# A graph message-passing layer on one core: slots ranked up to 110 chunks ahead, shorter last segments, and a new hand-over between steps

## The chip, the cores and the metric

The kernel runs on one core of a Trainium2 chip. Its instructions are spread over five engines that run side by side, each through its own queue in order: PE (matrix products), DVE (vector arithmetic), ACT (activations), POOL (GpSimd; here it issues the scattered writes) and SP (which here issues nearly all other DMAs). The metric is the time of one execution on the device, in microseconds; the median of several runs is compared. One further execution is recorded by the profiler, and takes longer than the others.

## The reference

Only what matters is kept. There are 12500 nodes of 128 features and 412500 edges sorted by `dst`; `src` is in no order.

```python
h = jnp.maximum(_layernorm(x, axis=-1), 0.0)
h = h @ W_in2f                                        # per node
Wij = ssp(edge_attr @ W_f1 + b_f1) @ W_f2 + b_f2      # per edge, 20 -> 128 -> 128
x_ij = h[dst] * (Wij * edge_weight[:, None])          # per edge
agg = segment_sum(x_ij, src, num_segments=12500)      # per node
out = x + ssp(agg @ W_o1 + b_o1) @ W_o2 + b_o2        # ssp(z) = softplus(z) - log 2
```

## The kernel before, in words

**Tiles and chunks.** The edges are cut into groups of 2048 and chunks of 512 (`CH`); there are 202 groups (`NG`) and 806 chunks (`NCH`). One round of the main loop, `step(k)`, works on chunk k and on its neighbours: it finishes message k, prepares chunk k+1 and starts the first stages of chunks up to six ahead. The program writes the order of every engine's instructions out by hand (`manual_schedule`): an instruction stands in its engine's queue where the Python code emits it. Pools of buffers set the waits: a tile name with `bufs=4` may be written again only when the readers of its fourth last use are done.

**Gathering h[dst].** `make_h` (L317) normalizes four tiles of 128 nodes at a time, multiplies by `W_in2f` and stores the product as three bfloat16 parts in DRAM (L369). As `dst` is sorted, a chunk needs only 32 neighbouring nodes. `rows` (L599) loads these as `near`; `window` (L741) compares on DVE where each edge falls, giving `at`; `pick` (L768) multiplies `at` by `near` on PE and so gives each edge its row; `picked` (L775) copies it on ACT into `hg`, scaled by the edge's weight (L780).

**The edge filter.** For two chunks at a time `hidden` (L648) multiplies the 20 attributes by `W_f1` into `z` and runs Abs and Exp on ACT; `hidden_log` (L660) runs Ln; `hidden_end` (L664) adds the positive part on DVE, giving `r`. `bias` (L748) writes the bias of the second layer into PSUM by an ACT copy (L757), and `value` (L760) adds `r @ W_f2` to it on PE. `v` and `picked` share three PSUM buffers.

**Scattering.** `message` (L784) multiplies `v` by `hg` on DVE into `o` (L791; four buffers of two chunks each), and POOL writes the rows of `o` with four indirect DMAs per chunk (L795) to a table in DRAM, `slots`. Each row goes to a slot of the block of 128 nodes to which its `src` belongs. The slot is found by counting: `blocks` (L671) makes a one-hot matrix of each edge's block on DVE, `rank` (L679) adds it to running counts on PE (`free`, L692, and L725 for the chunk before), `rank_end` (L696) reduces them on DVE (`top`, L697), and three small DVE operations make the slot (L717 to L721). Before, this is done six chunks ahead of the message (`LR`).

**Segments and sums.** The groups are dealt into segments (`SEGS`), each with its own table of `T` tiles of 128 slots per block (one more for blocks that hold the chunk's own nodes). Tables are cleared by SP beforehand (L1099). When a segment's last message is nine steps old, `Collect` starts: it loads tiles of the table (`m`, L833), compares each row's place with 0 to 127 on DVE (`to`, L844), multiplies on PE (`acc`, L857), and adds each four blocks ("a quad") to `agg` in SBUF (L880). These units are dealt over the steps by a plan of rates in the program, up to step 811. The sums of the last segment come behind the loop, together with `finish` (L397): for each quad `agg @ W_o1` on PE, four passes on ACT (L385, L386, L394, L395), on DVE the sum `r` (L420), `x + b_o2` (L423), on PE `r @ W_o2` (L427), on DVE the last sum (L431), and the store of the result.

**Queues.** Loads and stores share SP's queue, so a DMA that waits for a buffer or for data holds those behind it. On DVE, message k stands behind `blocks`, `hidden_end` and `window` of later chunks; on PE, the picks of chunk k+1 stand behind its values.

Of the kernel before, what the change touches and what calls it, by code (L numbers as in the profile page):

```python
# [22 lines left out]
SEGS = (88, 40, 30, 14, 14, 8, 8)  # L23
# [6 lines left out]
UT = 6  # L30
# [11 lines left out]
def gnn_kernel(  # L42
# [38 lines left out]
    class Segment:  # L81
# [4 lines left out]
        def __init__(self, k):  # L86
# [7 lines left out]
            mean = (SEGS[k] * TG * P - (own[1] - own[0])) / QT * P / N  # L94
# [32 lines left out]


    tables = [(0, QN)]
# [4 lines left out]
    for c in range(NC):  # L134
        n = c * CH * N // n_edges
        table_of.append(0 if n < QN - NEAR - P else min(n // QN, NQ - 1) + 1)
# [4 lines left out]
    bf1, nbf1, bo1 = (sbuf(n, [P, 1]) for n in ("bf1", "nbf1", "bo1"))  # L141
# [10 lines left out]
    bf12 = sbuf("bf12", [P, P])  # L152
    zero = sbuf("zero", [P, ZR * RW])
# [27 lines left out]
    def load_x(q):  # L181
        n = min(QT, NTILE - q * QT)
        full = min(n, N // P - q * QT)
        xb = ln.tile([P, QT, P], F32, name="xb")
        if full < n:
            nc.vector.memset(xb[:, full:n, :], 0.0)
            nc.sync.dma_start(xb[:N % P, full, :], x[q * QN + full * P:N, :])
        if full:
            nc.sync.dma_start(xb[:, :full, :], x[q * QN:q * QN + full * P, :]
                              .rearrange("(c p) f -> p c f", p=P))  # L190
        return xb
# [59 lines left out]

    def constants():
# [3 lines left out]
        first_load(0)  # L256
        nc.sync.dma_start(win, w_in2f)

        for j in range(NCHUNK):
            nc.sync.dma_start(wf1[32 * j:32 * j + RBF, :], w_f1)  # L260

        nc.scalar.preload_act_table_set("natural_log_exp_and_others")
        nc.scalar.dma_start(bf1, b_f1[:, None])
        nc.scalar.dma_start(wf2, w_f2)
        nc.scalar.dma_start(bf2, b_f2[None, :].to_broadcast([P, P]))
        make_identity(nc, ident)
        for _ in bounds(0, nc.gpsimd):
            pass

        prow_i = early_room[:WP, rows_at + 5 * NC:rows_at + 5 * NC + 1].bitcast(I32)  # L270
# [6 lines left out]
                                pattern=[[1, P]], channel_multiplier=-1)  # L277
        nc.gpsimd.memset(zero, 0.0)
# [8 lines left out]
        nc.vector.memset(bad, 0.0)  # L287
        nc.vector.memset(rel[:, NPART - 1, :], 0.0)
        nc.vector.memset(ones, 1.0)
        nc.vector.memset(none, 0.0)  # L290

        for t in range(QT):
            nc.vector.memset(turn[:, :, t:t + 1], -1.0 if t % 2 else 1.0)
        nc.vector.tensor_scalar(prow_i, prow_i, 7, None, op0=ALU.logical_shift_right)
        nc.vector.tensor_copy(prow, prow_i)
# [3 lines left out]

    def biases(psum):  # L300

        nc.vector.tensor_scalar(nbf1, bf1, -1.0, None, op0=ALU.mult)
        b12 = psum.tile([P, QT, P], F32, name="b12", tag="acc")[:, 0, :]
        nc.tensor.matmul(b12, bf1.to_broadcast([P, P]), wf2, start=True, stop=True)
        nc.vector.tensor_add(bf12, b12, bf2)

    def late_loads():
        nc.sync.dma_start(wo1, w_o1)
# [5 lines left out]
    quads = []  # L314


    def make_h(q, psum):  # L317

        n = min(QT, NTILE - q * QT)
        xb = early.pop(q, None)  # L320
        if xb is None:
            xb = load_x(q)
# [41 lines left out]
        for (b, rows), table in zip(tables, h3_t):  # L364
            lo = max(0, b - q * QN) // P
            hi = min(n, (b + rows - q * QN) // P)
            if lo < hi:
                r = q * QN + lo * P - b
# [3 lines left out]
                if b + rows == QN:  # L372
                    yield
            if q == NQ - 1:
# [4 lines left out]
            h3[q * QN:q * QN + n * P, :].rearrange("(c p) f -> p c f", p=P),  # L379
            hb[:, :n, :, :].rearrange("p c k f -> p c (k f)"))  # L380
        yield
# [15 lines left out]
    def finish(t0, n, sT, quad, psum):  # L397
# [13 lines left out]
        yield  # L411

        z = psum.tile([P, 2, CH], F32, name="z_out", tag="z")[:, 0, :n * P]
# [3 lines left out]
        softplus_parts(a_n, r_n, z, bo1)  # L417
        softplus_logs(a_n)
        yield
        nc.vector.tensor_add(r_n, r_n, a_n)  # L420
        for p, cs, rows in pieces:
            xi = xo[:p, cs, :]
            nc.vector.tensor_add(xi, xi, spread(bo2[:p, :], xi.shape[1]))  # L423
        yield
        v = psum.tile([P, QT, P], F32, name="v_out", tag="v", bufs=3)
# [92 lines left out]
    with tc.tile_pool(name="edge", bufs=2) as edge, tc.tile_pool(  # L518
# [46 lines left out]
        class Group:  # L565


            def __init__(self, g):
# [3 lines left out]
                if g % NB == 0:  # L572
                    f = edge.tile([P, NB, CH], F32, name="f")
                    for j in range(NCHUNK):
                        nc.sync.dma_start(f[32 * j:32 * j + RBF, :, :],
                                          f_t[g:g + NB, j].rearrange("b k n -> k b n"))
                    kept["f"] = f
                self.f = kept["f"][:, g % NB, :]
                i = g - self.seg.g0
                if i % SB == 0:  # L580
                    w = min(SB, ceil_div(self.seg.c1, NCHUNK) - g) * TG
                    cols = slice(g * TG, g * TG + w)
                    src_i = edge.tile([P, SB * TG], I32, name="src_i")
                    nc.sync.dma_start(src_i[:, :w], src_t[:, cols])
                    rcut = edge.tile([P, SB * TG], F32, name="rcut")
                    nc.sync.dma_start(rcut[:, :w], rcut_t[:, cols])
                    kept["cols"] = [w, src_i, rcut]
                self.cols = kept["cols"]
                self.at = slice(i % SB * TG, (i % SB + 1) * TG)
                if g == 0:  # L590
                    rel_store(0)
# [620 lines left out]
```

## Time and profile before

| | |
|---|---|
| median of 3 runs | 4227.72 us (4224.9 to 4232.52) |
| profiled execution | 5772.48 us |
| its span | 5770.8 us |
| busy in it: PE, DVE, POOL, ACT | 3877.3, 3382.9, 3103.5, 2715.3 us |
| first scatter starts | 29.44 us |
| last scatter starts | 5625.94 us |
| granted TensorE clock, mean | 0.718 |

Rows of the timeline give start, duration, engine, line, operation, output <- inputs, and in brackets how long the engine was idle just before and what ended the wait. "issue" means that nothing the profile shows was waited for; "remote" that the releaser could not be named. Rows of groups give the count, busy time, mean duration and the idle time in front. PE's durations are modelled by the profiler.

### The profile page before, as it was taken

To read this page: it belongs to the slowest core of one execution; us is meant where nothing else is said; L and a number is where in the kernel's file an instruction comes from. 1 tells how busy PE (TensorE), PEld (TensorE's weight loads), DVE (VectorE), ACT (ScalarE), POOL (GpSimd) and SP (SyncE) were. 2 spreads that over 40 slices of the span, in tenths; PEclk is the share of its full clock that TensorE was granted. 3 is DMA by queue.
4 is the path that set the end of the run, shared out by engine and by line. 5 is a ranking of instruction groups with operands and counts; after the bars stand their busy time and mean duration, and the time that the engine had idled before them with its cause. 6 is when DMAs were issued, how large, how long until landed. Compare 5 with 4: busy or idle time off the path is not lost. (4 is left out here: it accounts for less than half of the span.)

```text
span 5770.8 us, 71871 instructions
## 1 busy us (share of the span) xinstructions
PE 3877.3 (67%) x21576; PEld 2912.2 (50%) x21576; DVE 3382.9 (59%) x6726; ACT 2715.3 (47%) x5490; POOL 3103.5 (54%) x3244
## 2 busy tenths in 40 slices
PE   5556555556555555577777777777777777777778
PEld 3333333333333333356655666566566665655557
DVE  5555555555444444466665666666666666566767
ACT  4455554555444444444444444444444444444444
POOL 5555555555555555555555555555555555555550
PEclk7665566565556566578777787788877788787879
DMA  5444443343333333255664554655555555555547
GB/s 150 138 135 141 130 141 119 115 137 104 99 89 87 106 109 87 82 152 161 188 183 137 158 160 144 190 163 157 160 168 173 154 150 178 165 141 153 145 126 215
DMA packets 515581, 820.80 MB, mean 142 GB/s; under 512 B 177074, under 2 KB 312870, under 8 KB 515186
## 3 DMA queue, kind: packets, MB, share of 16 engines
q1 hardware_dynamic: 411586, 602.85, 37.4%
q0 software_dynamic: 103168, 213.15, 11.2%
q8 instruction: 176, 2.88, 0.2%
q14 instruction: 219, 1.79, 0.1%
q10 hardware_dynamic: 432, 0.13, 0.0%
HBM read 419.09 MB, written 396.64 MB: 141 GB/s over the span
## 5 line engine op out<-in xcount | busy, mean ns | idle before, releaser
L795 POOL DMA_INDIRECT slots<-o,slot x3224 | 3100.3, 962 | 2522.6 <-DVE o L791 1605.2
L764 PE MATMUL v<-wf,r 128*128 128x128 f32 x6448 | 1209.4, 345 | 527.4 <-ACT a L657 207.3
L857 PEld LDWEIGHTS acc<-to,m 128*128 128x128 f32 x8132 | 1249.1, 238 | 577.1 <-issue 280.8
L857 PE MATMUL acc<-to,m 128*128 128x128 f32 x8132 | 1342.0, 329 | 271.0 <-DVE agg L880 136.4
L764 PEld LDWEIGHTS v<-wf,r 128*128 128x128 f32 x6448 | 1077.6, 251 | 850.7 <-issue 301.8
L780 ACT ACTIVATE hg<-picked,rcut 128x128 f32<-128x128 f32 x3224 | 913.1, 365 | 1256.6 <-remote 801.2
L697 DVE TENSOR_REDUCE top<-free 128x4 f32<-128x392 f32 x806 | 451.5, 560 | 1650.5 <-remote 990.2
L757 ACT ACTIVATE v<-bf 128x512 f32<-128x512 f32 x804 | 478.0, 595 | 1212.9 <-DVE o L791 888.5
L653 PE MATMUL z<-f,wf 20*128 20x512 f32 x1612 | 661.1, 881 | 406.9 <-DVE r L668 242.4
L844 DVE TENSOR_TENSOR to<-count_ps,m 128x512 f32<-128x512 f32 (+3 forms) x824 | 644.7, 806 | 255.3 <-remote 109.3
L772 PE MATMUL picked<-near,at 96*128 96x128 bf16 x3224 | 398.5, 257 | 495.3 <-ACT hg L780 317.4
L668 DVE SCALAR_TENSOR_TENSOR r<-z,nbf,a 128x1024 f32<-128x1024 f32 x403 | 516.2, 1281 | 242.3 <-ACT a L662 136.3
L656 ACT ACTIVATE a<-z,bf 128x1024 f32<-128x1024 f32 x403 | 454.0, 1127 | 400.4 <-remote 267.8
L772 PEld LDWEIGHTS <-at 96*128 96x128 bf16 x3224 | 315.5, 118 | 558.1 <-issue 531.3
L791 DVE TENSOR_TENSOR o<-v,hg 128x512 f32<-128x512 f32 x806 | 547.8, 680 | 16.8 <-ACT hg L780 12.8
L744 DVE TENSOR_TENSOR at<-count_ps,rel 96x512 bf16<-96x512 f32 x806 | 545.3, 677 | 0.0
L653 PEld LDWEIGHTS z<-f,wf 20*128 20x128 f32 x1612 | 174.6, 241 | 620.9 <-issue 428.9
L662 ACT ACTIVATE a<-a,half 128x1024 f32<-128x1024 f32 x403 | 468.1, 1162 | 0.0
L673 DVE TENSOR_TENSOR inb<-count_ps,blk 128x392 f16<-128x392 f32 x806 | 445.9, 554 | 0.0
L657 ACT ACTIVATE a<-a 128x1024 f32<-128x1024 f32 x403 | 425.8, 1057 | 12.8
L725 PE MATMUL free<-inb,rest_of 128*128 128x392 f16 x806 | 335.3, 416 | 117.6 <-issue 46.9
L692 PE MATMUL free<-inb,after 128*128 128x392 f16 x806 | 335.9, 417 | 17.4 <-issue 13.6
(108 smaller groups left out, 1142.5 us busy)
## 6 DMA issues: line engine op xcount, KB each, us to landing
m<-slots SPq DMA_DIRECT2D x311, 387.0 KB
m<-slots SPq DMA_DIRECT2D x317, 258.0 KB
rel<-rel_d SPq DMA_DIRECT2D x202, 384.0 KB
m<-slots SPq DMA_DIRECT2D x172, 322.5 KB
slots<-o,slot POOLq DMA_INDIRECT x3224
slots<-zero SPq DMA_DIRECT2D x96, 387.0 KB
slots<-zero SPq DMA_DIRECT2D x64, 516.0 KB
f<-in_f_t SPq DMA_DIRECT2D x404, 80.0 KB
```

The costliest lines, as they stand in the source:

```text
L653: nc.tensor.matmul(z[:, k, :], wf1[rows, :], self.f[rows, :], start=True, stop=True)
L662: nc.scalar.activation(a, a, AF.Ln, bias=half, scale=0.5)
L668: nc.vector.scalar_tensor_tensor(r, z, nbf1, a, op0=ALU.max, op1=ALU.add)
L744: nc.vector.tensor_tensor(at, prow_ps.to_broadcast([WP, CH]), self.rel[:, c, :], op=ALU.is_equal)
L757: nc.scalar.activation(v, spread(bf12, QT), AF.Copy)
L764: nc.tensor.matmul(v[:, i, :], r[:, i * P:(i + 1) * P], wf2, start=False, stop=True, skip_group_check=True)
L772: nc.tensor.matmul(ps[:, i, :], at[:, i * P:(i + 1) * P], near, start=i == 0, stop=i == QT - 1, skip_group_check=True)
L780: nc.scalar.activation(hg[:, i, :], ps[:, i, :], AF.Copy, scale=self.rcut[:, j:j + 1])
L791: nc.vector.tensor_mul(o[:, :, :P], v, hg)
L795: put = nc.gpsimd.indirect_dma_start(out=views[j % VIEWS], out_offset=bass.IndirectOffsetOnAxis(ap=self.slot[:, j:j + 1], axis=0), in_=o[: ...
L844: nc.vector.tensor_tensor(to[:, :n, :], count_ps[:, None, :].to_broadcast([P, n, P]), self.m[u][:, :n, P:].to_broadcast([P, n, P]), op=ALU ...
L857: nc.tensor.matmul(self.acc[b // QT][:, i, :], m[:, j, :P], to[:, j, :], start=t == 0, stop=t == self.seg.tiles(b) - 1)
```

## The change

Ranking is cut loose from the rest of a chunk. A new class `Places` holds what concerns slots (columns, `blocks`, `rank`), `Group` the rest. `ahead(k)` says how far ranking has come at step k: about six chunks ahead in the first rounds, then rising by a quarter to half a chunk per step up to 110 (`LEAD`), so that the last 110 steps have no ranking. Buffers for slots and places grow accordingly. `free`, the PSUM bank of the counts, becomes a second bank for `acc` when ranking is over (`sums_tile`).

The nine segments end in 3, 3 and 4 groups, where seven ended in 8 and 8. Loads of sums have at most four tiles (`UT`) and nine buffers; the compares take buffers from the pool of `make_h`. The plan of rates gives the last 110 steps half as much again.

Within a step, the message comes first. `picked` gets two PSUM buffers of its own and is filled two chunks ahead; `v` gets one. The bias of `v` is added by a PE matmul of a bfloat16 matrix with three rows of ones on the bias in three bfloat16 parts. Abs, Exp and Ln of `hidden` run together, one step after `z`. At the start the first tile of 128 nodes goes through `make_h` alone, then three, then four each; loads and constants come in another order, some from ACT's queue. In `finish`, the bias `b_o1` is folded in (`nbo1`; `b_o1 @ W_o2` is added to `b_o2`), one ACT pass and one DVE pass less are needed, and `x + b_o2` moves to GpSimd.

```diff
-SEGS = (88, 40, 30, 14, 14, 8, 8)
+SEGS = (88, 41, 25, 18, 12, 8, 3, 3, 4)
+LEAD = 110
-UT = 6
+UT = 4
+    made_h = [(0, 1), (1, QT - 1)]
+    made_h += [(t, min(QT, NTILE - t)) for t in range(QT, NTILE, QT)]
...
     def finish(t0, n, sT, quad, psum, tag="v", bufs=3, z=None):
+        for p, cs, rows in pieces:
+            xi = xo[:p, cs, :]
+            nc.gpsimd.tensor_add(xi, xi, spread(bo2[:p, :], xi.shape[1]))
...
-        softplus_parts(a_n, r_n, z, bo1)
+        nc.scalar.activation(a_n, z, AF.Abs, bias=bo1)
         softplus_logs(a_n)
         yield
-        nc.vector.tensor_add(r_n, r_n, a_n)
-        for p, cs, rows in pieces:
-            xi = xo[:p, cs, :]
-            nc.vector.tensor_add(xi, xi, spread(bo2[:p, :], xi.shape[1]))
+        nc.vector.scalar_tensor_tensor(r_n, z, nbo1, a_n, op0=ALU.max, op1=ALU.add)
...
+            def hidden_log(self, c):
+                z = self.pair[c]
+                a = quad.tile([P, 2, CH], F32, name="a", bufs=2)
+                nc.scalar.activation(a, z, AF.Abs, bias=bf1)
+                nc.scalar.activation(a, a, AF.Exp, scale=-1.0)
+                nc.scalar.activation(a, a, AF.Ln, bias=half, scale=0.5)
...
-            def value(self, c, v):
+            def value(self, c):
+                v = psum.tile([P, QT, P], F32, name="v", bufs=1)
                 r = self.pair[c // 2 * 2][:, c % 2, :]
                 for i in range(QT):
                     nc.tensor.matmul(v[:, i, :], r[:, i * P:(i + 1) * P], wf2,
-                                     start=False, stop=True, skip_group_check=True)
+                                     start=i == 0, stop=False, skip_group_check=True)
+                nc.tensor.matmul(v.rearrange("p t f -> p (t f)"), ones_b, spread(bf12_p, QT),
+                                 start=False, stop=True, skip_group_check=True)
...
-                m = edge.tile([P, UT, RW], F32, name="m", bufs=5)
+                m = edge.tile([P, UT, RW], F32, name="m", bufs=9)
...
+        def sums_tile():
+            kept["banks"] = kept.get("banks", 0) + (made["rank"] == NCH - 1 and not ranked)
+            if kept["banks"] % 2:
+                return state_ps.tile([P, QT, P], F32, name="acc_b", tag="free")
+            return psum.tile([P, QT, P], F32, name="acc")
...
+        LATE = NCH - LEAD
+        def ahead(k):
+            lead = LR if k < LEAD_AT else min(LR + (k - LEAD_AT) // 2, LEAD)
+            return min(k + lead, k + 1 + (k + 1) * (LR - 1) // RAMP, NCH - 1)
...
+        def pace(k):
+            return k + 0.5 * max(0, k - LATE)
+        def cost(c, u):
+            return c.units[u][1] * c.units[u][3] + 3.3 * c.ends(u)
```

The body of `step(k)` after the change, in steady state (from step 20 on), without the branches of the first rounds:

```python
part("rows", min(k + LW, 2 * k + 3, served()), rows)   # SP: near
group(...); slots_of(...)                              # SP: f, rcut, rel, src
g.message(c, vs.pop(k), hgs.pop(k))                    # DVE: o; POOL: four scatters
keep()                                                 # DVE: agg
slots()                                                # DVE: top and slots of the last rank
if ahead(k) > made["rank"] + 1: rank()                 # PE: free
if waiting(): add(2)                                   # PE: acc, in the last 110 steps
part("blocks", ...); part("end", ...); keep()          # DVE: inb, r, agg
part("window", k + 3, window)                          # DVE: at
part("pick", k + 2, pick)                              # PE: picked
vs[k + 1] = g.value(c)                                 # PE: v
if waiting(): add(1)                                   # PE: acc
for seg, u in units: seg.load(u + AHEAD)               # SP: m
hgs[k + 1] = g.picked(c, ps.pop(k + 1))                # ACT: hg
part("log", ...)                                       # ACT: Abs, Exp, Ln
for c, u in units: c.compare(u); summed.append((c, u)) # DVE: to
while made["rank"] < ahead(k): slots(); rank()         # DVE, PE
part("hidden", k + LZ, pairs(hidden))                  # PE: z
add(...)                                               # PE: acc
```

## The prediction

> **What bounds the kernel now.** I read the page first: its span, and the costliest group of each engine.
>
> ```profile
> span 5770.8 us, 71871 instructions
> PE 3877.3 (67%) x21576; PEld 2912.2 (50%) x21576; DVE 3382.9 (59%) x6726; ACT 2715.3 (47%) x5490; POOL 3103.5 (54%) x3244
> L795 POOL DMA_INDIRECT slots<-o,slot x3224 | 3100.3, 962 | 2522.6 <-DVE o L791 1605.2
> ```
>
> No engine looks full, and the profiled execution (5772.48 us) is 1545 us longer than the median of the runs (4227.72). So shares of this span mislead. The timeline of POOL alone says more:
>
> ```profile
> 71.69 0.96 POOL L795 DMA_INDIRECT slots<-o,slot  x1 [0.30 <-issue]
> 72.96 0.96 POOL L795 DMA_INDIRECT slots<-o,slot  x1 [0.31 <-issue]
> 74.23 0.96 POOL L795 DMA_INDIRECT slots<-o,slot  x1 [0.30 <-issue]
> ...
> 5625.94 0.96 POOL L795 DMA_INDIRECT slots<-o,slot  x1 [0.30 <-issue]
> ```
>
> Each scatter takes 0.96 us and the next starts 1.266 us after it, whenever its data is there (five in six of the 3223 gaps lie between 1.260 and 1.268). A chunk has four scatters, so POOL cannot pass a chunk in less than 5.06 us. 3223 x 1.266 = 4080 us. From the first scatter (29.4) to the last (5625.9) the profile has 5596 us, so 1516 us of it are POOL waiting. The longest waits look like this:
>
> ```profile
> 1508.05 1.14 ACT L780 ACTIVATE hg<-picked,rcut 128x128 f32<-128x128 f32 x4 [5.82 <-remote]
> 1508.09 0.57 DVE L697 TENSOR_REDUCE top<-free 128x4 f32<-128x392 f32 x1 [6.49 <-remote]
> ```
>
> ACT and DVE stand still together behind PE, for a cause that the trace doesn't name. The runs without a profile have no room for them: 1.7 us outside the span + 29.4 head + 4080 scatters + 6.8 lost in the first rounds (below) leave 110 us for everything behind the last scatter, and the profile's last stage (below) takes 109.7. So I take the timed kernel to be POOL back to back, with a head, a tail, and hardly a gap between. DVE may run ahead of POOL by the four buffers of `o`, two chunks each: some 7 chunks or 35 us. That cushion also hides the 33 us (5628 to 5661 in the profile) of the next to last segment's sums, which the timed run does while POOL works off its queue.
>
> The head, from the timeline:
>
> ```profile
> 16.05 0.39 SPq L369 DMA_DIRECT2D h<-hb  x1
> 18.68 1.52 SPq L608 DMA_DIRECT2D near<-h  x2
> 26.60 1.28 DVE L668 SCALAR_TENSOR_TENSOR r<-z,nbf,a 128x1024 f32<-128x1024 f32 x1 [6.46 <-ACT a L662]
> 28.47 0.68 DVE L791 TENSOR_TENSOR o<-v,hg 128x512 f32<-128x512 f32 x1
> 29.44 1.13 POOL L795 DMA_INDIRECT slots<-o,slot  x1 [25.45 <-DVE o L791]
> ```
>
> The first message stands behind the second pair's `r` on DVE, which waits 6.46 us for ACT. The first scatters of chunks 0 and 6 start at 29.44 and 66.63: 37.2 us for six chunks where POOL needs 30.4, so 6.8 lost.
>
> The tail, busy times by stage (columns: window, its length, then PE, PEld, DVE, ACT, POOL, clock, DMA share, GB/s):
>
> ```profile
> 5661.00:5755.00 94.00, 87.70 (x606) 72.86 (x607) 85.11 (x137) 55.14 (x88) 0.00 (x0) 1.00 0.84 252
> 5755.00:5771.00 16.00, 7.76 (x53) 6.31 (x51) 7.98 (x17) 6.55 (x12) 0.00 (x0) 0.93 0.34 100
> ```
>
> 24.5 quads of blocks in 94 us: 3.84 us each, with DVE, PE and DMA all near full.
>
> **Two rules of the skill.** The Trainium skill, "TensorE: Matmul & The Clock Gate", section "What's actually happening", says that the array's clock is at half unless recent activity releases it. The trace agrees: 0.60 granted between 200 and 1800 us, where PE has little to do, 0.78 from 2300 to 5600, 1.00 in the tail. So PE's busy time is no fixed cost, and I price PE at the full clock it gets when it is the engine in need. "GPSIMD Engine Reference", section "3.1 Elementwise", gives 4497 ns for a float32 two-input add of 2048 elements on GpSimd; my estimate for 512 elements is a quarter, 1.1 us. Before shows no such add; the nearest rows are DVE's own add (654 ns) and a POOL memset of 1032 elements (963 ns). I take 1.1, with 0.65 and 2 as ends.
>
> **The change part by part.**
>
> *The scatters* stay 3224, in the same form: 0 at the bound.
>
> *Bias of v.* 804 ACT copies (595 ns, 478 us) go. In their place PE gets 806 matmuls of 512 bfloat16 columns. No row is the same; z's records of 512 columns come at 1.06 us for four at full clock, so about 0.25 us each. +0.25 us of PE per chunk, hidden under POOL.
>
> *PE per chunk at full clock*, from a stretch near 4205 us without a stop: four value matmuls 0.89, four picks 0.23, two of `free` 0.34, z 0.53, and 0.222 for each tile of the sums. Before: 2.0 us early, and with 8.5 tiles 3.9 us in the collecting stage. After: 2.2 and about 4.1. In the last 110 chunks no rank is left, but the built order has 10.6 to 12.2 tiles per chunk: 4.3 to 4.6. All stay under 5.06.
>
> *DVE per chunk*, from the built order at the rows' start-to-start times: before 3.3 early, 4.3 to 4.7 in the collecting stage. After: 3.8 between chunks 100 and 220 (1.25 to 1.5 ranks a step, each 0.48 + 0.50 us and its slot arithmetic), 4.6 just past chunk 361, 4.4 until 696, 4.0 until 780, 4.8 in the last 26. Under 5.06 too. The rank moved ahead is the same work earlier; the cover is POOL. Were it gone, each 0.1 us per chunk would cost 81 us.
>
> *Waits.* `v` has one buffer instead of a share of three: value(k+1) on PE waits for message k on DVE; behind it stand z and the tiles, for which agg on DVE waits. But value and message make a loop of 0.89 + 0.25 + 0.68 us, far under 5.06. `picked` has two buffers and is filled a step earlier; hidden's three ACT passes (1.13 + 1.06 + 1.16) come one step later as a block. I cost these at 0, ends -10 to +60 in all.
>
> *SP.* More loads of sums (1201 instead of 824 in the built order, 276 MB instead of 269), clears 155 MB instead of 145; nine buffers instead of five let them start earlier. 18 MB more in 4200 us is 4 GB/s: hidden.
>
> *Head.* The first tile alone shortens normalization by three bn pairs (1.2 us), three scalings (0.8), three transposes (0.9), three h matmuls (1.5) and four shorter copies (about 1.3): 5.7 us on the way to the store of h. But the store now stands on SP behind the reload of rel, which waits for its own store: about 10.0 instead of 16.05, near some 2.6 us later, pick near 14.5. DVE's queue then is the later one: shift, column arithmetic (13 instructions, 3.3 us), inb, at, top, slot, r, three bn pairs, the second tile's scaling, then the message: about 22.0, scatter at 22.5. Gain 7, ends 3 and 11. The 6.46 us wait is gone, because message stands first in its step; what is late next is DVE itself.
>
> *First rounds.* DVE has 4.2 us per chunk in the first 20, value and picks come ahead; loss 2 instead of 6.8. Gain 5.
>
> *Tail.* Last segment of 4 groups, one tile per block: in the built order 27 compares instead of 49 behind the flag. Per quad on DVE before two compares, agg, r, xo + b_o2, xo + v: 6 x 0.604 us + a gap = 3.74; after 4 x 0.604 = 2.42. PE 4 x 0.222 + 0.53 + 0.89 = 2.3; GpSimd 1.1 and idle otherwise. Bytes per quad: sums 0.264 MB instead of 0.528, x and out 0.262 each: 0.788 MB. At 252 GB/s (this stage) to 296 (512-byte packets at 18.5 bytes/ns on 16 engines) that is 3.1 to 2.66 us. So DMA is last: 2.85 us, 70 us instead of 94; one ACT and one DVE pass less in the end, 1 us. Gain 25, ends 12 and 35. The segment before it leaves 20 compares and 22 aggs behind the last message, 25 us at 0.604: still under POOL's 35.
>
> Sum: 7 + 5 + 25 = 37 us. The profiled time without its 1516 us of waits and the 30 us hidden in a timed run is 4227, the median; so 4227.7 - 37 = 4191 us.
>
> **Rivals.**
>
> A, slower: the collecting stage leaves POOL's shade. One mechanism: PE, in order, holding value behind tiles that wait for agg or a compare, so that a chunk takes longer than POOL's 5.06 us. It decides at 5.06 + 37/445 = 5.15 us mean over the 445 chunks from 361 on. For it: 4.6 to 4.8 us on both engines near the end, and a half clock doubles PE. Against it: more work raises the clock, and ranks leave the late chunks. At 5.20: +62 - 37, 4253 us.
>
> B, more gain: the timed scatter is shorter than in the profile, say 1.25 us, so before holds 3223 x 0.016 = 52 us of gaps in the collecting stage, where DVE has 4.7 us, and the change closes them: 4140 us.
>
> C, tail unchanged: GpSimd's adds at 2 us or more, or loads of 516-byte rows at under 210 GB/s, keep a quad at 3.8 us: 4227.7 - 12 = 4216 us. For it: DMA at 0.84 of its time already.
>
> That slots aren't found ahead is no rival: the built order has no rank in the last 110 steps.
>
> **Numbers.** Forecast 0.66 (4172 to 4206 its own range), A 0.15, B 0.10, C 0.09. 4191 stands. The range leaves out A and the far part of B: 4140 to 4236. 0.2% is 8.5 us, about what a measurement can tell from no change. Faster: 0.66 + 0.10 + most of C = 0.81; same 0.04 of C's upper part and A's lower; slower 0.15.
>
> **What would show it.** Right: scatters still 1.266 us apart, first near 22.5 us; no ACT row into v; the quads of the tail near 2.9 us with DMA over 0.85; no `inb` or `top` in the last 110 chunks. Wrong: a pitch other than 1.266, POOL waiting longer for `o` in the collecting stage than before, PE over 95% busy at full clock there (A), or tail quads at 3.8 us with `xo` on POOL in front of DVE (C).

## The result, and the profile after

The changed kernel takes 4237.32 us (4235.02 to 4244.55, 20 runs) where the kernel before takes 4227.86 (4223.55 to 4234.53, 20 runs): ratio 1.0022 [1.0015, 1.0029]. A second comparison (e10) gives 1.0013 [1.0007, 1.002]. The forecast was 4191 us and faster, with a range of 4140 to 4236; it is slower by about 0.2%, just outside the range.

The forecast was read from a profile of 5770.8 us. To compare like with like, the kernel before was profiled again (e1): that execution took 4226.24 us, no longer than the runs without a profile beside it (median 4227.36). So it was not the profiler that made the first one long; it ran at a granted clock of 0.718, e1 at 0.828. The comparisons of stages below are with e1. First the pages, each with the span, the engines' busy time and the scatters' group. After:

```profile
span 4236.4 us, 75523 instructions
PE 3423.6 (81%) x22612; PEld 2582.9 (61%) x22612; DVE 3427.0 (81%) x7238; ACT 2317.5 (55%) x4670; POOL 3159.3 (75%) x3276
L854 POOL DMA_INDIRECT slots<-o,slot x3224 | 3123.9, 969 | 1004.1 <-issue 757.3
```

Before (e1):

```profile
span 4224.5 us, 71871 instructions
PE 3359.7 (80%) x21576; PEld 2576.0 (61%) x21576; DVE 3373.6 (80%) x6726; ACT 2678.2 (63%) x5490; POOL 3099.2 (73%) x3244
L795 POOL DMA_INDIRECT slots<-o,slot x3224 | 3096.0, 960 | 1010.7 <-issue 777.7
```

In both, the idle time in front of the scatters is nearly all the 0.30 us that stands between any two of them: 3224 x 0.30 = 967 us of the 1004 or 1011. (The profile puts three quarters of it down to "issue" and spreads the rest over whatever ended last.) The waits for a message are short, and a good part of them is the wait for the first one (total, times, longest); after, then before (e1):

```profile
POOL slots L854 <- DVE o L850: 42.2, 70, 16.6
POOL slots L795 <- DVE o L791: 47.9, 67, 25.6
```

So both are bound by POOL back to back, as the forecast took it. But one scatter takes 969 ns in place of 960. The timeline of POOL, in the middle of the main loop (start, duration, idle time before): after,

```profile
2000.65 0.97 POOL L854 DMA_INDIRECT slots<-o,slot  x1 [0.30 <-issue]
2001.92 0.97 POOL L854 DMA_INDIRECT slots<-o,slot  x1 [0.30 <-issue]
2003.19 0.97 POOL L854 DMA_INDIRECT slots<-o,slot  x1 [0.31 <-issue]
```

and before (e1),

```profile
2000.61 0.96 POOL L795 DMA_INDIRECT slots<-o,slot  x1 [0.30 <-issue]
2001.87 0.96 POOL L795 DMA_INDIRECT slots<-o,slot  x1 [0.30 <-issue]
2003.14 0.96 POOL L795 DMA_INDIRECT slots<-o,slot  x1 [0.31 <-issue]
```

The pitch, here and below, is the mean of all gaps between the starts of two scatters that are under 1.32 us (some 3180 of 3223 in these two). It is 1.2628 us before and 1.2716 after, the same in every part of the loop, from the first 40 scatters on. 8.8 ns x 3223 = 28 us. With the first and the last scatter and the span, each kernel divides into three parts:

| us | head: to the first scatter | first to last scatter | tail: behind the last scatter's start | span |
|---|---|---|---|---|
| before (e1) | 29.6 | 4080.1 | 114.8 | 4224.5 |
| after | 21.7 | 4110.4 | 104.3 | 4236.4 |
| difference | -7.9 | +30.3 | -10.5 | +11.9 |

The head and the tail gain 18 us, and the scatters take 30 back. Head and end of the scatters in the timeline of after:

```profile
21.68 1.13 POOL L854 DMA_INDIRECT slots<-o,slot  x1 [16.61 <-DVE o L850]
...
4132.12 0.97 POOL L854 DMA_INDIRECT slots<-o,slot  x1 [0.30 <-issue]
```

The tail gains less than forecast. Two stretches of it by busy time (length, then PE, PEld, DVE, ACT, POOL, clock, DMA share, GB/s), after:

```profile
4139.00:4184.00 45.00, 43.22 (x285) 35.27 (x286) 40.12 (x66) 31.71 (x47) 15.26 (x12) 1.00 0.81 217
4184.00:4207.00 23.00, 17.99 (x117) 14.17 (x116) 15.71 (x26) 12.10 (x19) 7.60 (x6) 1.00 0.75 211
```

and the main stretch of before (e1):

```profile
4115.00:4209.00 94.00, 88.32 (x605) 74.17 (x606) 84.12 (x135) 55.11 (x88) 0.00 (x0) 0.98 0.87 257
```

In the first stretch of after PE is nearly full, and the quads come every 2.69 us. From 4184 us on nothing is full: PE 18.0 of 23, DVE 15.7, DMA 0.75. The timeline there shows what is waited for (a GpSimd row in front of each DVE row):

```profile
4184.51 1.27 POOL L447 TENSOR_TENSOR xo<-xo,bo 128x512 f32<-128x512 f32 x1 [2.52 <-DMA xo<-in_x]
...
4185.81 0.69 DVE L467 TENSOR_TENSOR xo<-xo,v_out 128x512 f32<-128x512 f32 x1 [0.96 <-POOL xo L447]
...
4188.14 1.26 POOL L447 TENSOR_TENSOR xo<-xo,bo 128x512 f32<-128x512 f32 x1 [2.37 <-DMA xo<-in_x]
...
4189.44 0.69 DVE L467 TENSOR_TENSOR xo<-xo,v_out 128x512 f32<-128x512 f32 x1 [1.09 <-POOL xo L447]
```

DVE waits for GpSimd's addition, GpSimd waits 2.4 to 2.5 us for the load of x, and this quad takes 3.63 us (4185.81 to 4189.44); the others there take 3.5 to 4.7. Why the load is late stands in the waits of SP's queue, from 4132 us on (total, times, longest):

```profile
SPq L443 <- DMA out<-xo: 43.9, 19, 4.0
```

The load (L443) waits for a store of the result to land, since `xo` has six buffers and one is free only when its last store is done.

### The profile page after: what moved, and what is told of

It is laid out like the page before. It is cut to its first block, busy times and chain, and to the rows that moved or that the text cites. A ratio compares the mean times of both kernels' runs of the same rounds, so it can differ in the third digit from the quotient of the medians.

```text
span 4236.4 us, 75523 instructions
## 1 busy us (share of the span) xinstructions
PE 3423.6 (81%) x22612; PEld 2582.9 (61%) x22612; DVE 3427.0 (81%) x7238; ACT 2317.5 (55%) x4670; POOL 3159.3 (75%) x3276
## 5 line engine op out<-in xcount | busy, mean ns | idle before, releaser
L819 PE MATMUL v<-wf,r 128*128 128x128 f32 x6448 | 1071.4, 318 | 367.4 <-DVE o L850 365.7
L819 PEld LDWEIGHTS v<-wf,r 128*128 128x128 f32 x6448 | 934.6, 223 | 405.0 <-DVE o L850 393.8
L926 PEld LDWEIGHTS acc<-to,m 128*128 128x128 f32 x6940 | 873.8, 202 | 197.7 <-issue 108.5
L926 PE MATMUL acc<-to,m 128*128 128x128 f32 x6940 | 926.8, 290 | 25.5 <-DVE to L913 19.6
L913 DVE TENSOR_TENSOR to<-count_ps,m 128x512 f32<-128x512 f32 (+2 forms) x1202 | 674.7, 607 | 23.4 <-DMA m<-slots 23.2
L788 PE MATMUL z<-f,wf 20*128 20x512 f32 x1612 | 537.3, 747 | 183.1 <-DVE r L804 181.1
L804 DVE SCALAR_TENSOR_TENSOR r<-z,nbf,a 128x1024 f32<-128x1024 f32 x403 | 513.7, 1275 | 26.3 <-ACT a L797 26.3
L848 DVE COPY o<-place 128x8 f32<-128x8 f32 x403 | 79.0, 196 | 475.1 <-DMA slots<-o,slot 474.4
L830 PEld LDWEIGHTS <-at 96*128 96x128 bf16 x3224 | 267.0, 107 | 212.9 <-issue 70.8
L830 PE MATMUL picked<-near,at 96*128 96x128 bf16 x3224 | 349.7, 237 | 13.9 <-DVE at L810 12.5
L821 PE MATMUL v<-bf_p,ones_b 128*128 128x512 bf16 x806 | 352.2, 437 | 0.0
```

What stands on the lines that cost most here:

```text
L788: nc.tensor.matmul(z[:, k, :], wf1[rows, :], self.f[rows, :], start=True, stop=True)
L804: nc.vector.scalar_tensor_tensor(r, z, nbf1, a, op0=ALU.max, op1=ALU.add)
L819: nc.tensor.matmul(v[:, i, :], r[:, i * P:(i + 1) * P], wf2, start=i == 0, stop=False, skip_group_check=True)
L830: nc.tensor.matmul(ps[:, i, :], at[:, i * P:(i + 1) * P], near, start=True, stop=True)
L913: nc.vector.tensor_tensor(to[:, :n, :], count_ps[:, None, :].to_broadcast([P, n, P]), self.m[u][:, :n, P:].to_broadcast([P, n, P]), op=ALU ...
L926: nc.tensor.matmul(self.acc[b // QT][:, i, :], m[:, j, :P], to[:, j, :], start=t == 0, stop=t == self.seg.tiles(b) - 1)
```

## The experiments

The experiments ran on five chips. On the second, fourth and fifth the kernel before takes 5747 to 5844 us at a granted clock of 0.72, on the first and third 4227 to 4232 at 0.83; so a time is compared only with the kernel before on the same chip. The first profile of the kernel before has the low clock. e1, e6 and e7 are one execution each, which is also the profiled one.

| run | chip | added GpSimd operations | pitch, us | us, median | ratio to before |
|---|---|---|---|---|---|
| e1 | first | none | 1.2628 | 4226.24 | |
| e2 | first | none | 1.2629 | 4207.53 | 0.9956 [0.9942, 0.9969] |
| e3 | first | addition | 1.2716 | 4220.92 | 0.9983 [0.9977, 0.999] |
| e4 | first | addition | 1.2715 | 4255.4 | 1.0068 [1.0054, 1.0081] |
| e5 | second | addition | 1.2712 | 5740.02 | 0.9969 [0.9943, 0.9995] |
| e6 | second | copy | 1.2743 | 5774.68 | |
| e7 | second | addition | 1.2715 | 5308.27 | |
| e8 | second | addition | 1.2745 | 5281.23 | 0.9192 [0.9165, 0.922] |
| e9 | third | none | 1.2629 | 4207.07 | 0.9938 [0.9924, 0.9951] |
| e10 | third | addition | 1.2716 | 4237.06 | 1.0013 [1.0007, 1.002] |
| e11 | third | addition | 1.2727 | 4254.92 | 1.0055 [1.004, 1.0071] |
| e12 | third | copy | 1.2716 | 4255.16 | 1.0055 [1.0037, 1.0074] |
| e13 | fourth | none | 1.2652 | 5840.27 | 0.9993 [0.9973, 1.0013] |
| e14 | fourth | memset | 1.2625 | 5841.18 | 0.9989 [0.9968, 1.001] |
| e15 | fourth | addition and copy | 1.2624 | 5828.64 | 0.9962 [0.994, 0.9984] |
| e16 | fourth | none | 1.2624 | 5367.22 | 0.9181 [0.9148, 0.9214] |
| e17 | fifth | addition and copy | 1.2624 | 5837.8 | 0.9996 [0.9979, 1.0013] |
| e18 | fifth | addition and copy | 1.2623 | 5363.29 | 0.9181 [0.9157, 0.9204] |

### First question: the tail, and what lengthens the scatters (e1 to e4)

Theory X: the tail of after is held by the loads of x, which wait for a free buffer. Theory G: it is held by GpSimd's addition.

**e1**, the kernel before, unchanged.

> The kernel before, unchanged, profiled once more, because its first profile took 5772 us and its timed runs 4228. Theory P (the scatter's pitch is a property of the program): POOL starts a scatter each 1.265 us here too, where the changed kernel has 1.272, and a span near 4226 us divides into a head of 29.4, some 4084 for the scatters, and a tail of about 112. Rival Q (the pitch belongs to the execution or the chip): 1.272 us here as well; then head, scatters and tail must be 29.4 + 4100 + 97, and the tail before was shorter than I took it to be.

It gave the profile at the higher clock that is used above. Its pitch is 1.2628 us, so Q falls: the 1.272 of the changed kernel doesn't come with every execution. But it is not the 1.2651 of the first profile of the same kernel either, so up to 2.3 ns of pitch come with the execution or the chip. Gaps beyond the pitch add up to 10 us between the first and the last scatter.

**e2**, the addition back on VectorE, behind `r`:

```diff
-            nc.gpsimd.tensor_add(xi, xi, spread(bo2[:p, :], xi.shape[1]))
...
+            nc.vector.tensor_add(xi, xi, spread(bo2[:p, :], xi.shape[1]))
```

> The changed kernel with x + b_o2 on DVE again, behind r in each quad, and GpSimd free of it. Theory X (what holds the tail is the load of x, which waits on SP until the store that last used its buffer of six has landed): DVE gets 25 x 0.60 = 15 us more work, but the x load still paces the quads at about 3.6 us, so the time stays within 5 us of the changed kernel, 4237 +- 5. Rival G (GpSimd's adds of 1.27 us hold the tail): the add leaves the path, 8 to 15 us faster, 4222 to 4229.

4207.53 us: 30 us under the changed kernel, which neither theory had foreseen. The tail is the same (104.4 us), though not for one reason: its first thirteen quads take 3.05 us in place of 2.69, with DVE busy for 30.00 of 30.00 us from 4130 on, and the later ones again wait for the load of x. SP's queue waits for a store about as long as in the changed kernel:

```profile
SPq L443 <- DMA out<-xo: 43.3, 19, 3.2
```

So that wait does not come from GpSimd's additions; e3 decides between X and G. The gain is all in the scatters, 4083.7 us from first to last in place of 4110.4. The page of e2:

```profile
span 4209.7 us, 75520 instructions
L853 POOL DMA_INDIRECT slots<-o,slot x3224 | 3095.2, 960 | 1006.1 <-issue 764.9
```

960 ns, as before. The 26 additions that were taken away all stand behind the last scatter, and yet the scatters ahead of them became shorter. This is the origin of theory P as it is meant from here on: the program has a longer pitch because it holds a GpSimd addition. (In e1, P was only that the pitch belongs to the program.)

**e3**, nine buffers for x:

```diff
-        xo = quad.tile([P, QT, P], F32, name="xo", bufs=6)
+        xo = quad.tile([P, QT, P], F32, name="xo", bufs=9)
```

> The changed kernel with nine buffers for x instead of six, nothing else. Theory X: the load of x no longer waits for the store, quads go at 2.7 us (the pace of DVE) to the end, 24.5 x 2.7 = 66 us instead of 87 minus what the last loads cost: 10 to 18 us faster, 4219 to 4227. Rival G: no change, within 3 us of 4237. Rival D (DMA bandwidth holds it): at most 5 us faster.

4220.92 us; the tail is 93.4 us in place of 104.3, the pitch as in after. X holds, and G falls: the additions are still on GpSimd. Two last sums show the quads, which stay at 2.69 us for the first eighteen:

```profile
4185.29 0.68 DVE L467 TENSOR_TENSOR xo<-xo,v_out 128x512 f32<-128x512 f32 x1
...
4187.98 0.68 DVE L467 TENSOR_TENSOR xo<-xo,v_out 128x512 f32<-128x512 f32 x1
```

Fifty microseconds of its tail by busy time, and the longest wait of SP's queue in the tail:

```profile
4150.00:4200.00 50.00, 50.00 (x333) 40.92 (x334) 46.69 (x74) 37.73 (x56) 23.04 (x19) 1.00 0.97 275
```

```profile
SPq L470 <- DVE xo L467: 27.0, 20, 3.4
```

The wait of the loads for a store is gone from the list; PE is busy without a break and the DMAs at 0.97. The queue now waits where it should, for the sum that a store is to write.

**e4**, the segments of before:

```diff
-SEGS = (88, 41, 25, 18, 12, 8, 3, 3, 4)
+SEGS = (88, 40, 30, 14, 14, 8, 8)
```

> The changed kernel with the segments of before (88, 40, 30, 14, 14, 8, 8), so that the last segment has eight groups and two tiles per block; all else as changed. If the shorter last segments bring what the prediction gave them: about 15 us slower than the changed kernel (24.5 quads x 4 more tiles and one more compare, 0.6 us of DVE each), near 4252. If the tail is held by x's buffers alone (theory X) the extra compare is partly hidden: 0 to 8 us slower.

4255.4 us, tail 123.9. That is near the 4252 of the first expectation; the buffers of x alone (0 to 8 us slower) do not explain it. The short last segments are worth 19.6 us of the tail. It also shows that the rest of the change makes the tail longer than that of before by 9.1 us (123.9 against 114.8); so the tail adds up: 114.8 + 9.1 - 19.6 = 104.3. Where most of the 9.1 lies, the trace shows: a quad takes 4.18 us, where e1 has 3.74, and from the first of the last sums to the last one 93.9 us pass in place of 87.8. In each quad DVE waits 0.9 us for ACT before `r`:

```profile
4165.73 0.75 DVE L459 SCALAR_TENSOR_TENSOR r_out<-z_out,nbo,a_out 128x512 f32<-128x512 f32 x1 [0.90 <-ACT a_out L455]
...
4169.91 0.75 DVE L459 SCALAR_TENSOR_TENSOR r_out<-z_out,nbo,a_out 128x512 f32<-128x512 f32 x1 [0.89 <-ACT a_out L455]
```

Which edit brings this wait was not tried.

### Second question: is it the addition (e5 to e8, e10 to e12)?

**e5**, the kernel before with one small addition behind the last scatter:

```diff
+    probe = sbuf("probe", [P, 2])
...
+        nc.vector.memset(probe, 0.5)
...
+            nc.gpsimd.tensor_add(probe[:, 0:1], probe[:, 0:1], probe[:, 1:2])
             go(0)
```

> The kernel before with one addition of two columns of 128 numbers by GpSimd, behind the last scatter and ahead of the last tail; nothing else is changed. Theory P (a program that holds a two-input GpSimd operation has a longer pitch of scatters all along): pitch 1.271 to 1.272 us in place of 1.2628 from the first scatter on, +28 us, about 4255 us. Theory L (the longer pitch comes with the way in which the changed kernel lies in memory or in its queues, and e2 differs from it in that too): pitch 1.263, time within 3 us of the kernel before.

**e6**, a copy in its place:

```diff
+            nc.gpsimd.tensor_copy(probe[:, 0:1], probe[:, 1:2])
             go(0)
```

> The same as the kernel with one tiny addition behind the last scatter, with a one-input copy of a column of 128 numbers by GpSimd in its place. Theory P: the kind matters, a copy with one input leaves the pitch at 1.263, about 4228 us. Rival (any operation of GpSimd that works on data behind the scatters lengthens the pitch): 1.271 to 1.272, about 4255 us. Under theory L 1.263 too, but then the tiny addition shows 1.263 as well.

**e7**, e2 with the small addition among the constants, ahead of all scatters:

```diff
+        nc.gpsimd.tensor_add(probe[:, 0:1], probe[:, 0:1], probe[:, 1:2])
```

> The changed kernel with the addition of x and b_o2 back on VectorE (as in e2) and one tiny addition of two columns by GpSimd among the constants, ahead of the first scatter. Theory P in the form 'the program holds one, wherever it stands': pitch 1.2716, about 4236 us. In the form 'an addition that is still to come behind the scatters': pitch 1.263, about 4208 us. Theory L: 1.263.

**e8** is not the kernel that its expectation describes: it keeps GpSimd's additions, and so it is the changed kernel with nine buffers and with loads of x four quads ahead:

```diff
-        xo = quad.tile([P, QT, P], F32, name="xo", bufs=6)
+        xo = quad.tile([P, QT, P], F32, name="xo", bufs=9)
...
-            go(0)
+            for j in range(4):
+                go(j)
...
-                    go(q + 1)
+                    go(q + 4)
```

> The changed kernel with the addition of x and b_o2 on VectorE behind the output bias (as in e2), nine buffers for x in the tail (as in e3) and the loads of x issued four quads ahead in place of one. If the two gains of e2 and e3 add up (-30 and -16 us at most, of which the tail's share was 11 us) and the early loads let VectorE run its quads at 2.7 to 3.3 us throughout: 4190 to 4198 us, tail 85 to 94 us, faster than both kernels. Rival (VectorE with the additions of x and b_o2 back is the tail's bound at once, 3.3 us a quad, and the loads are hidden): tail 100 to 104, about 4207 us as in e2.

These four ran at the low clock, where the scatters wait for the engines ahead of them, so 28 us of pitch do not show in the time (e5 is even a little under the kernel before), and no absolute time that was expected applies. The pitch shows: 1.271 to 1.275 in all four, wherever the addition stands. That is what P expects, and not L, which expected 1.263 in e5 and e7. A copy does it as well as an addition, against P's expectation for e6. But no kernel without an addition or copy was profiled on this chip; the nearest one to compare with is the first profile of before, at a like clock, with 1.2651.

They show something else: e7 and e8 take 8% less than the kernel before. The scatters' group of e8, beside the one in the prediction:

```profile
L854 POOL DMA_INDIRECT slots<-o,slot x3224 | 3134.7, 972 | 2019.6 <-DVE o L850 1120.3
```

POOL waits 1120 us for a message, where it waited 1605 in the first profile of before: 485 us, about the whole gain of 466 (5747.16 less 5281.23). At the low clock these variants of the change are worth a great deal, since there POOL waits for its data. The changed kernel without a further edit was not run there, and which part of the change brings the gain was not tried.

**e9** is told below. **e10**, the changed kernel again:

> The changed kernel as it is, beside the kernel before on the same chip. At a granted clock as in the first four experiments: 1.0022 of the kernel before, pitch 9 ns above that of a kernel with no GpSimd addition. At the low clock of e5 to e8 (0.72 in the kernel before): 0.92 to 0.93 of the kernel before, as in e7 and e8, since there the scatters wait for the engines ahead of them and the change gives the slots a longer lead.

It came as expected for the higher clock: 1.0013 of the kernel before, pitch 1.2716.

**e11** is the kernel of e5 and **e12** that of e6, on a chip with the higher clock.

> The kernel before with one tiny GpSimd addition behind the last scatter (as in e5). Theory P: the pitch is longer than that of the kernel before by 5 to 9 ns from the first scatter on, +15 to +29 us, 4243 to 4257 us where the kernel before takes 4228. Theory L: pitch and time as before, within 3 us.

> The same with a one-input copy by GpSimd in place of the addition (as in e6). Theory P, in the form that e6 showed (any operation with an input in memory, not the addition alone): pitch longer by 9 ns, about +29 us, 4257 us where the kernel before takes 4228. Rival (e6's pitch came with its execution, not with the copy): pitch and time as before.

Here the pitch sets the time. One addition of two columns makes the kernel before slower by 23.3 us (4254.92 against 4231.62), and a copy by 23.5. (The kernel before has no profile on this chip. Were its pitch e9's, 1.2629, the longer one would cost 28 to 32 us; were it the 1.2651 of its first profile, 21 to 25.) The addition runs once, behind all scatters, but the timeline of e11 has the long pitch in the middle of the loop:

```profile
2000.51 0.97 POOL L797 DMA_INDIRECT slots<-o,slot  x1 [0.30 <-issue]
2001.79 0.97 POOL L797 DMA_INDIRECT slots<-o,slot  x1 [0.30 <-issue]
2003.06 0.97 POOL L797 DMA_INDIRECT slots<-o,slot  x1 [0.31 <-issue]
```

So it is not that an addition stands in the scatters' way: what the program holds counts. On this chip e9, with no addition, has 1.2629, and e10, e11, e12 have 1.2716 to 1.2727.

### Third question: which programs (e13 to e15, e17)

**e13**, the small addition by VectorE, on the same buffer; **e14**, a GpSimd memset of it; **e15**, addition and copy by GpSimd:

```diff
# e13
+            nc.vector.tensor_add(probe[:, 0:1], probe[:, 0:1], probe[:, 1:2])
# e14
+            nc.gpsimd.memset(probe[:, 0:1], 0.25)
# e15
+            nc.gpsimd.tensor_add(probe[:, 0:1], probe[:, 0:1], probe[:, 1:2])
+            nc.gpsimd.tensor_copy(probe[:, 0:1], probe[:, 1:2])
```

> The kernel before with the tiny addition of e11 made by VectorE in the same place, on the same small buffer. Theory P (a GpSimd operation of a further kind in the program): pitch 1.263, time of the kernel before within 4 us. Theory L (the small buffer, its preset or the layout behind it): pitch 1.272, +23 us as in e11.

> The kernel before with one GpSimd memset of a column of 128 numbers behind the last scatter; memsets by GpSimd are among the constants of both kernels already. If a further kind counts: pitch 1.263, time of the kernel before within 4 us. If any GpSimd operation behind the scatters counts: 1.272, +23 us.

> The kernel before with a tiny addition and a tiny copy by GpSimd behind the last scatter. If each further kind adds a step: pitch 1.281, about +50 us. If there is one step for any number of kinds: 1.272, +23 us as in e11 and e12.

On this chip (low clock again) e13 has 1.2652, like the first profile of before, and e14 1.2625: neither has the long pitch, so here the small buffer, its preset and a memset behind the scatters do not bring it. But e15 has 1.2624. Neither of its two expectations, 1.272 or 1.281, came true: with an addition and a copy together the pitch is short. Theory P, that an addition or copy in the program is enough, falls as it was stated. Theory K took its place: the set of kinds of GpSimd operations decides, and these two together give the short pitch. (E, its rival: the short pitch came with the execution.) As no program on this chip has the long pitch, e13 and e14 are no full controls for e11 and e12 either.

**e17**, the kernel of e15 again:

> The kernel of e15 again: the kernel before with a tiny addition and a tiny copy by GpSimd behind the last scatter. Theory K (the set of kinds of GpSimd operations in the program sets the pitch; addition and copy together give the short one): pitch within 1 ns of the kernel before (1.263), and its time within 4 us. Theory E (e15's short pitch came with its execution): pitch 1.272, +23 us where the kernel before takes 4228 to 4232.

1.2624 again, on another chip, as K expects. Its time, 0.9996 of the kernel before, says nothing at the low clock.

### The combined versions (e9, e16, e18)

**e9**, the addition on VectorE, nine buffers, loads of x four quads ahead (the edits of e2 and e8 together):

> The changed kernel with the addition of x and b_o2 on VectorE (as in e2), nine buffers for x in the tail and its loads issued four quads ahead; no GpSimd operation beside the scatters and the constants. Where the granted clock is that of the first four experiments: theory P (no GpSimd addition, pitch 1.263) with the tail's gain of e3 (11 us) on top of e2: 4194 to 4200 us, tail 90 to 95 us, faster than both kernels. Rival (with the additions back on VectorE its own work is the tail's bound): pitch 1.263, tail 100 to 105, about 4207 us. If the pitch is above 1.268, theory P falls.

Pitch 1.2629, as P (and K) expect; but the tail is 107.5 us, so here the rival was right. Fifty microseconds of the tail:

```profile
4130.00:4180.00 50.00, 47.71 (x300) 36.96 (x298) 50.00 (x83) 33.74 (x51) 0.00 (x0) 1.00 0.70 195
```

DVE is busy for 50.00 of 50.00 us: with the additions back it bounds this part of the tail. The quads hold 3.05 us for eighteen where e2 has thirteen. But the first last sum comes 26.3 us behind the last scatter (20.1 in e2), perhaps since four loads of x now stand ahead of loads of sums on SP's queue, and two late quads take 5.6 us. So the tail is no shorter. Nine buffers without the early loads were not tried with the additions on DVE. At 0.9938 [0.9924, 0.9951] e9 is faster than the kernel before and, 30 us under e10 on the same chip, faster than the changed kernel. Its absolute time is that of e2 (4207.07 and 4207.53).

**e16**, the bias by PE, in three bfloat16 parts (`bo2_p` is made as `bf12_p` is), no addition elsewhere, nine buffers; of its edit only the matmul is shown:

```diff
+        nc.tensor.matmul(v[:, :n, :].rearrange("p t f -> p (t f)"), ones_b, spread(bo2_p, n),
+                         start=False, stop=True, skip_group_check=True)
```

> The changed kernel with b_o2 added by one bfloat16 matmul of 128x512 a quad into the sums on PE (three bfloat16 parts of the bias, as the change does for the bias of v), no addition of x and b_o2 elsewhere, and nine buffers for x. Pitch 1.263 by theory P. If PE bounds the tail with nine buffers (e3 showed it busy throughout most of it): 26 matmuls of about 0.38 us add up to 10 us to a tail of 93, 100 to 104, about 4205 us. If DVE or the transfers bound it: tail 90 to 95, about 4197 us.

**e18**, e3 with a small copy behind the last scatter:

```diff
-        xo = quad.tile([P, QT, P], F32, name="xo", bufs=6)
+        xo = quad.tile([P, QT, P], F32, name="xo", bufs=9)
...
+            nc.gpsimd.tensor_copy(probe[:, 0:1], probe[:, 1:2])
             go(0)
```

> The changed kernel with nine buffers for x (as in e3), its additions of x and b_o2 on GpSimd, and one tiny copy by GpSimd behind the last scatter. Theory K: pitch 1.263 in place of e3's 1.2716, so 28 us less than e3's 4221: about 4193 us where the kernel before takes 4228, ratio 0.991 to 0.993. Theory E: pitch 1.272, about 4221 us, ratio 0.998. At the low clock of e5 to e8 the pitch alone tells.

Both ran at the low clock. The pitches, 1.2624 and 1.2623, are those that P or K expects: in e18 the changed kernel's additions are still there, and a copy that is added to them goes with the short pitch. Both times are 0.918 of the kernel before. Of their tails (110.7 and 109.3 us) little can be said at that clock, and whether e18 would take 4193 us on a chip with the higher clock is not shown.

**What stays open.** On the first and third chips, programs with an addition or a copy have a pitch 9 to 10 ns above those with neither, and a longer time; that is shown, by programs that ran side by side (e1 and e2 against e3 and e4, e9 against e10 to e12). On the fourth and fifth chips no program with one of the two alone was run. So that both together give the short pitch by themselves (K) has two chips and three programs for it, but it can't be told from these two chips having the short pitch whatever the program holds. Nor does the program alone settle the pitch: the same kernel has 1.2651 and 1.2628 (before, e1), 1.2712 and 1.2727 (e5, e11), 1.2743 and 1.2716 (e6, e12). These differences of up to 2.7 ns, and e13's 1.2652 beside 1.2625 on one chip, stay unexplained; the long and the short pitch are at least 6 ns apart all the same.

## Why the prediction was wrong

**The scatters: the step that failed.** "*The scatters* stay 3224, in the same form: 0 at the bound." The count and the form are right, and POOL back to back is the bound; but the pitch rose by 8.8 ns, +28 us over 3223 gaps. The addition on GpSimd was priced for what it takes itself (1.1 us each, in the tail), and its effect on the scatters was put at nothing without a reason. e2 takes it away and gets 30 us back; e11 adds one to the kernel before and costs 23. Why a scatter takes longer in a program that holds an addition stays open. The note of 1.266 us as something to check ("Wrong: a pitch other than 1.266") was the right place to look.

**The tail: direction right, pace and wait wrong.** Gain 25 forecast, 10.5 measured. The short segments gave 19.6 (e4). The forecast took a quad at the pace of its bytes, 2.85 us, with PE at 2.3. The DMAs could move the bytes faster than that: in e3 a quad takes 2.69 us with PE busy without a break, since `agg @ W_o1` takes PE some 0.9 us where the forecast put 0.53. But the loads go in order, and a load of x needs a buffer whose store has landed. With six buffers the quads take 3.5 to 4.7 us in the later part; nine (e3) keep 2.69 and bring 11 us more, 21.4 of the 25 in all. *SP* was costed as hidden from the volume of its traffic alone, and this wait in its queue was not looked for. Rival C had this outcome in part ("keep a quad at 3.8 us"), though for slow additions or slow loads of sums; the DMA share was 0.75 there. The addition itself: the Trainium skill, "GPSIMD Engine Reference", section "3.1 Elementwise", led to 1.1 us as an estimate, and the trace has 1.27 for 128x512; it is not the bound.

**Head: right.** Gain 7 forecast, 7.9 measured; first scatter at 21.68 where 22.5 was expected.

**First rounds: wrong by 7.** Gain 5 forecast. Over the first 80 gaps, the time beyond the pitch is 2.9 us in e1 and 5.2 in after (2.4 in e10): no gain, and no loss that is clear of the spread between two executions. The 6.8 us that were to shrink came from a profile at the low clock.

**Bias of v, PE, DVE, waits: right at 0.** Beyond the pitch, all gaps between the first and last scatter make 12.0 us of 4110.4 (10.2 in e1), so neither PE nor DVE left POOL's shade: rival A is false. Rival B's scatter was indeed shorter at the higher clock (1.2628), but there were no 52 us of gaps to close.

**The sum.** 7 + 5 + 25 + 0 = 37 us forecast; 7.9 - 2.3 + 10.5 - 28.4 = -12.3, which is the -11.9 of the spans but for 0.4 us of other gaps. The tail's error of 14.5 us would have left a kernel that is faster by about 16; the sign came from the scatters. That the parts of before added up to its median within a microsecond was in part luck: in e1 the scatters with their gaps take 4080 us where the forecast has 4087, and the tail 115 where it has 110.

## What to carry to other kernels

Where one engine runs the same instruction thousands of times back to back, compare that instruction's duration to the nanosecond before and after an edit, even of an edit elsewhere, and on the same chip, as the same program differed by up to 2.7 ns between two chips here: 9 ns in 969 were 28 us, more than all that the change gained. A small piece of work that is moved to the engine that sets the pace should be tried alone, and on another engine beside it, before a larger change carries it along. And in a load, compute, store pipeline, count how long a buffer stays taken until its store has landed: six buffers cost 11 us in a tail of 104 where neither PE, DVE nor the DMAs were full.

## What was not expected of the hardware

- With one GpSimd addition of two columns, or copy of one, in the kernel before, run once behind all scatters (e11, e12), the 3224 indirect DMAs ahead of it have a pitch of 1.2727 or 1.2716, where a kernel without one on the same chip (e9) has 1.2629; the time is 23 us longer than that of the kernel before. The Trainium skill, "GPSIMD Engine Reference", section "2.1 Instruction dispatch", says that the engine finds the code for each instruction by software, in a table of functions; that a program's other operations change what an instruction costs it does not say, and no run here shows the cause.
- With an addition and a copy both in the program, the pitch was 1.2623 to 1.2624 on two chips, where no program with one of them alone was run.
- The same program takes 4227 to 4232 us on two chips and 5747 to 5844 on three others, at granted clocks of 0.83 and 0.72. Between 2300 and 4000 us PE was granted 0.77 and was busy for 1257 us in the first profile of before; in e1 it was granted 0.94 and was busy for 1457. Whether the chip, or the work itself that comes faster, sets the level is not shown. At the higher clock the changed kernel and its variants e2, e3 and e9 stand between 0.994 and 1.002 of the kernel before; at the low clock its variants e8, e16 and e18 stand at 0.918 to 0.919.
